# Normed rows moved to blocked tiles within SBUF, and transfers placed behind weight fetches, in a cross-attention and expert-FFN kernel

## The chip, the cores and the metric

One Trainium2 chip, one core. The metric is the device time of one execution in microseconds; the kernel before was timed in three runs. One profiled execution gives the page and the trace.

## What is computed

All in float32. Two steps, each added to x (8 batches of 1024 rows of 1024 numbers):

```python
def xattn(h, mem, mask):           # h = layernorm(x); mem: 8 x 64 x 1024
    scores = einsum('bsd,bmd->bsm', h, mem) / sqrt(D)
    attn = softmax(where(mask, scores, -1e30))
    return einsum('bsm,bmd->bsd', attn, mem)

def ffn(h, weight, lora_A, lora_B, router_w):   # h = layernorm(x)
    base = h @ weight.T                          # 1024 x 1024
    top2 = the two largest of softmax(h @ router_w.T), made to sum to 1   # 8 experts
    Ax = einsum('nd,erd->ner', h, lora_A)        # rank 16
    return base + einsum('ner,ne,eor->no', Ax, top2, lora_B) * 2

x = x + xattn(layernorm(x), ctx, mask)
x = x + ffn(layernorm(x), weight, lora_A, lora_B, router_w)
```

## The kernel before

The 8192 rows are 64 tiles of 128 rows. Two tiles make a pair, two pairs a quad. `first` does pairs 0 and 1 and prepares the weights; `quad(u)` is called for u = 2, 4, ... 30. Inside it, `u` and `v` are the pairs whose large product with the weights is made; `n`, `m` are the next two, whose attention, norm and turning are done meanwhile; `a`, `b` are the last two, to which the low-rank part is added before they are stored; `f`, `g` come after `n`, `m` and are loaded, turned and scored. `r` is a tile of a pair.

The large product is done with fewer block products, at two levels. A quad makes seven products, in the order 2, 5, 4, 1, 6, 7, 3 (`joint(i, u, ...)`), and each of them is seven parts of two matmuls 128x128 by 128x290 (four records in the profile, since each float32 matmul shows as two). The 34 columns beyond 256 carry a share of the low rank and the router. A part's result is read out of PSUM into T or xt by VectorE, or by ScalarE where `copy` says so (L906 to L946). `joint_sums` (L867) makes a product's operands on GpSimd (POOL); `t_add` (L835) adds T to xt there; `sums_1_2` (L711) makes the sums of a pair.

Three of the seven weight operands of a product are sums of weight blocks that lie in DRAM, in pieces of 290 KB. `fetch()` (L775) brings the next piece on SyncE's queue (SP) into one of four buffers (`q`), and `joint` calls it three times: after its second part, its fourth and its last. The order is fixed (L768), so that the fetches of product 5 bring two pieces of product 4 and one of product 1, those of product 4 two of product 1 and one of 6, those of product 6 two of product 7 and one of 3, and so on. The second part of a product needs its piece 4, the fourth part piece 2, the last part piece 3. In the trace the pieces are `q_w` and `q_t`, by the name of the weight block.

All DMAs are issued by SP, in the order of the program; the other engines follow the order of the program too (`manual_schedule`). What SP waits for holds up all behind it.

VectorE can transpose blocks of 32x32 alone. So rows that are to be turned must lie blocked: the tile's partitions 32q to 32q+31 hold column group q (256 columns) of the rows of all four row groups t. x is loaded a second time in this form (`xs`, `load_xs`, L115, four DMAs of 128 KB per tile) and turned by `att_turn_tile` (L444). The normed rows `h` (`f_rows`, L330, on ScalarE) are written to DRAM (`hd`, one DMA of 512 KB per tile) and read back blocked (`hs`, four DMAs of 128 KB per tile) by `norm_send` and `norm_fetch` (L589, L598), and `rt_turn_tile` (L619) turns them. `xs`, `h`, `hs` are tiles of one pool of four buffers of 4 KB per partition (`ring`, L66).

The attention memory of a batch serves four pairs. For every second quad, up to u = 22, a new one is read in blocked form (`load_ms`, L391, eight DMAs of 32 KB in runs of 128 bytes), turned and summed (`turn_mem`, L404) and centred (`centre_turned`, L412).

`turn_low_rank` (L695) turns the routed low-rank numbers of two pairs on TensorE: two transposes, a copy out of PSUM by ScalarE, two transposes, a copy; all four transposes write one bank. `lora_tile` (L952) adds them to xt by eight matmuls (`lo`) per pair. In a quad, SP and ScalarE are given:

- after product 2 and the attention of n and m: sums, squares and root of pair n (`f_sums`, `f_squares`, `f_std`), then `turn_low_rank`, then product 5 with `f_rows(n)` and its sending after the first part;
- `f_rows(m)`, the low rank of a and its stores, product 4, the low rank of b and its stores, load of f, product 1, load of g;
- product 6 with the turning of n, loads of `xs`, product 7 with the turning of m, loads of `xs`, product 3 with the turning of the xs of f; the xs of g are turned in product 2 of the next quad.

Of the kernel before, what the change touches and what calls it, by code (L numbers as in the profile page):

```python
# [17 lines left out]
P = 128  # L18
# [6 lines left out]
def kernel(  # L25
# [281 lines left out]
    def f_rows_steps(u: int):  # L307

        nm, std, of_f = fts.pop(u)
        rstd, nmr = of_f[:, 4], of_f[:, 5]  # L310

        def row(r: int):
            h = ring.tile([P, D], F32, tag="ring", name=f"h_{u}_{r}")
            hss.setdefault(u, []).append(h)
            nc.scalar.activation(
                halves(h), body(xts[u][r]), AF.Identity, bias=nmr[:, r, :], scale=rstd[:, r, :]
            )

        def one():
            nc.vector.reciprocal(rstd, std)  # L320
            tt(nmr, nm, rstd, ALU.mult)
            row(0)

        def two():
            row(1)
            norm_send(u)

        return one, two

    def f_rows(u: int, fetch: bool = True):  # L330
# [11 lines left out]
        norm_send(u, fetch)  # L342
# [48 lines left out]
    def load_ms(b: int):  # L391

        mt = memp.tile([P, KD, M], F32, tag="memT", name=f"memT_{b}_True", bufs=1)
        for q in range(4):
            for t in range(M // NB):
                nc.sync.dma_start(
                    out=mt[q * NB : (q + 1) * NB, :, t * NB : (t + 1) * NB],
                    in_=mem[b, t * NB : (t + 1) * NB, q * QD : (q + 1) * QD].rearrange(
                        "i (k c) -> i k c", c=NB
                    ),  # L400
                )
        mem_ts[b, True] = mt

    def turn_mem(b: int):  # L404

        mt = mem_ts[b, True]
        turn = mt.rearrange("p k (t i) -> p (k t) i", i=NB)
        nc.vector.transpose(turn, turn)
        mcs[b] = small.tile([P, M], F32, tag="of_k", name=f"of_k_{b}")
        nc.vector.tensor_reduce(mcs[b], mt.rearrange("p k m -> p m k"), AX.X, ALU.add)  # L410

    def centre_turned(b: int):  # L412

        of_k = mcs.pop(b)
        mt = mem_ts[b, True]
        means = bank_of(f"means_{b}")[:, :M]
        mm(means, ones, of_k, start=True, stop=True)
        tt(mt, mt, means.unsqueeze(1).to_broadcast([P, KD, M]), ALU.subtract)


    x_ts, scs, ps, pts, ros, hds, hss, rdens = {}, {}, {}, {}, {}, {}, {}, {}
# [167 lines left out]
    def norm_send(u: int, fetch: bool = True):  # L589

        hds[u] = dram.tile([2 * P, D], F32, tag="hd", name=f"hd_{u}")
        hs_in, hss[u] = hss[u], []
        for r in range(2):
            nc.sync.dma_start(out=hds[u][r * P : (r + 1) * P, :], in_=hs_in[r])
        if fetch:
            norm_fetch(u)

    def norm_fetch(u: int):  # L598
        for r in range(2):
            hs = ring.tile([P, 4, QD], F32, tag="ring", name=f"hs_{u}_{r}")  # L600
            load_blocked(hs, hds[u][r * P : (r + 1) * P, :])
            hss[u].append(hs)
# [277 lines left out]
    def joint(i: int, u: int, hooks, wide: int = HX, copy=None):  # L880
# [35 lines left out]
        def hook(step: int):  # L916
            for do in hooks.get(step, ()):
                do()
# [9 lines left out]
        fetch()  # L928
        read(v, 0, p4)
# [5 lines left out]
        fetch()  # L935
        read(u, 1, chain)
# [8 lines left out]
        fetch()  # L945
        tt(to(v), chain.unsqueeze(1).to_broadcast([P, 2, wide]), to(v), ALU.add)  # L946
# [29 lines left out]
    def first():  # L976
# [124 lines left out]
        load_xs(4)  # L1101
# [6 lines left out]
        f_rows(2)  # L1108
        low_rank_tile(1, 0)
# [6 lines left out]
        sum_3(1)  # L1116
        quarter_sums("t1", t1)
        load_ms(1)
# [20 lines left out]
        att_turn(4)  # L1139
# [4 lines left out]
        centre_turned(1)  # L1144
# [4 lines left out]
        end = joint_plain(2, 1, {0: lambda: product(1, 8)})  # L1149
# [6 lines left out]
        load_xs(5)  # L1156
# [3 lines left out]
        for _ in range(4):  # L1160
            fetch()
        x_stats(5)
# [12 lines left out]
    def quad(u: int):  # L1175
# [4 lines left out]
        far = f < NP  # L1180
        prev = u > 2
# [3 lines left out]
        next_mem = f + 2 < NP and (f + 2) % PPB == 0  # L1185
        vector, scalar = nc.vector.tensor_copy, nc.scalar.copy

        def nothing(*_):
            pass

        hooks = {}
        if more:
            att_sc([n, m])
            att_rstd(n)
            att_rstd(m)
            hooks[1] = [lambda: att_exp([n, m])]
        if far:
            load_xs(g) if not prev else nothing()
            if not prev:
                hooks[2] = [lambda: att_turn(f)]  # L1200
            hooks[3] = [lambda: att_turn_tile(g, 0)]
            hooks[5] = [lambda: att_turn_tile(g, 1)]
# [35 lines left out]
        if next_mem:  # L1238
            load_mask((f + 2) // PPB)
            load_ms((f + 2) // PPB)  # L1240
        if prev:
            turn_low_rank(a, b)

        hooks = {}
        if more:
            hooks[1] = [lambda: f_rows(n)]
        joint(5, u, hooks, wide, vector)
        if more:
# [3 lines left out]
            f_rows(m)  # L1252
# [3 lines left out]
        if prev:  # L1256
            for r in range(2):
                lora_tile(a, r)
                store(a, r)

# [3 lines left out]
        joint(4, u, {}, wide)  # L1264
        joint_sums(6, u)
        if prev:
            for r in range(2):
                lora_tile(b, r)
                store(b, r)
        if far:  # L1270
            load_xt(f)
# [3 lines left out]
        joint(1, u, {}, wide, scalar)  # L1275
# [4 lines left out]
        if far:  # L1280
            x_stats(f)
            load_xt(g)
        if not more:
            for r in range(2):
# [99 lines left out]
```

## Time and profile before

| what | value |
|---|---|
| median of three runs | 1369.92 us (1362.94 to 1375.46) |
| profiled execution, its own time | 1374.05 us |
| span in its trace | 1372.2 us |
| mean granted TensorE clock | 0.922 |
| TensorE matmuls busy | 84% of the span |
| VectorE, POOL, ScalarE busy | 57%, 56%, 41% |
| DMA traffic | 274.34 MB, 200 GB/s |

A row of the waits names the engine and line that waited, then what released it, the sum in us, how often and the longest. In the list of SP's queue SPq is SyncE issuing DMAs. `jc` and `j` are PSUM banks of the products, `lo` those of the low rank, `trw` that of the turned low rank, `L801` is the matmul of a block. The stretch from 645 to 728 us, one quad (u = 14) from the end of its readouts to the end of the next, is used throughout.

### The profile page before, as it was taken

Reading aid. Unit: us, or ns where it says so; the run is one execution under the profiler, and the core shown is the slowest. Engines: PE = TensorE matmul, PEld = TensorE weight load, DVE = VectorE, ACT = ScalarE, POOL = GpSimd, SP = SyncE. Lnnn points to the kernel's source line nnn. Section 1 sums busy time; section 2 is a strip of 40 time slices with the busy share of each in tenths; the row PEclk is TensorE's granted clock in tenths of the full one; section 3 lists DMA queues with packets and bytes.
Section 4 is the critical chain, followed back from the end, with each engine's and each line's share of the span. In section 5 each row is a group of like instructions: output and inputs, shape, how many; then the busy total and the mean of one; then the engine's idle time right before and its main releaser. Section 6 shows DMA issues by size and latency. Waiting matters only on the chain.

```text
span 1372.2 us, 16976 instructions
## 1 busy us (share of the span) xinstructions
PE 1151.1 (84%) x4968; PEld 791.7 (58%) x4968; DVE 787.5 (57%) x1829; ACT 555.9 (41%) x1116; POOL 761.7 (56%) x837
## 2 busy tenths in 40 slices
PE   8978788987888878888988888888888798878988
PEld 6444565655656646555665555656555565555766
DVE  6864456574664746647475464754647466363554
ACT  4663534434353253543345433354533445323110
POOL 0487364583644736556384554836448375463844
PEclk9998898998999999899899999989999899889999
DMA  9889483966839569394874839658395783827534
GB/s 221 212 257 277 151 245 113 306 157 196 254 105 305 143 188 274 107 310 124 262 220 151 270 99 309 180 174 273 108 299 148 223 263 107 269 70 240 143 118 127
DMA packets 218443, 274.34 MB, mean 200 GB/s; under 512 B 33392, under 2 KB 166512, under 8 KB 218352
## 3 DMA queue, kind: packets, MB, share of 16 engines
q1 hardware_dynamic: 218352, 273.26, 67.2%
q8 instruction: 41, 0.67, 0.2%
q14 instruction: 50, 0.41, 0.1%
HBM read 201.94 MB, written 71.25 MB: 199 GB/s over the span
## 4 chain that ended last, share of the span: by engine, by line
PE 46%; DMA 16%; DVE 11%; POOL 11%; ACT 9%; issue 3%; SPq 3%; DVEq 0%; ACTq 0%; POOLq 0%
PE j L801 20%; PE jc L801 18%; PE lo L791 7%; DMA q_w<-q_w 5%; DMA q_t<-q_t 5%; POOL xt L839 3%; ACT junk L296 3%; DVE xt L544 3%; DMA xt<-in_x_dram 2%; SPq L85 2%; DMA xs<-in_x_dram 2%; DVE xt L912 1%; DVE xs L448 1%; ACT junk L286 1%; POOL s L716 1%
## 5 line engine op out<-in xcount | busy, mean ns | idle before, releaser
L839 POOL TENSOR_TENSOR xt<-xt,T 128x580 f32<-128x580 f32 (+1 forms) x180 | 247.9, 1406 | 193.3 <-DVE T L912 193.3
L801 PE MATMUL jc<-q_t,s_j 128*128 128x290 f32 (+1 forms) x480 | 144.0, 423 | 60.6 <-DVE T L912 44.5
L912 DVE TENSOR_TENSOR T<-j,T 128x290 f32<-128x290 f32 (+1 forms) x180 | 76.0, 443 | 162.0 <-PE j L801 152.3
L801 PE MATMUL jc<-q_w,s_j 128*128 128x290 f32 (+1 forms) x360 | 115.4, 447 | 43.3 <-DMA q_w<-q_w 40.2
L801 PE MATMUL j<-w,s_j 128*128 128x290 f32 (+1 forms) x480 | 143.2, 422 | 8.2 <-DVE xt L912 6.5
L801 PEld LDWEIGHTS jc<-q_t,s_j 128*128 128x128 f32 x480 | 92.0, 197 | 98.1 <-DVE T L912 54.3
L875 POOL TENSOR_TENSOR s_j<-hA 128x256 f32<-128x256 f32 x30 | 22.2, 740 | 215.4 <-PE jc L801 215.4
L801 PEld LDWEIGHTS j<-w,s_j 128*128 128x128 f32 x480 | 95.9, 202 | 43.1 <-POOL s_j L876 10.4
L801 PEld LDWEIGHTS jc<-q_w,s_j 128*128 128x128 f32 x360 | 71.1, 205 | 73.6 <-issue 48.6
L801 PE MATMUL j<-t,s_j 128*128 128x290 f32 (+1 forms) x360 | 108.0, 424 | 0.0
L791 PE MATMUL lo<-lb_sb,axwt 128*128 128x512 f32 x240 | 107.8, 592 | 0.0
L510 ACT ACTIVATE s<-s,of_s 128x64 f32<-128x64 f32 x64 | 21.5, 337 | 200.5 <-DVE of_s L501 200.5
L912 DVE TENSOR_TENSOR xt<-j,xt 128x290 f32<-128x290 f32 (+1 forms) x180 | 78.1, 444 | 31.0 <-PE j L801 31.0
L339 ACT ACTIVATE h<-xt,of_f 128x1024 f32<-128x1024 f32 x60 | 71.2, 1234 | 55.2 <-DVE of_f L335 55.2
L910 ACT COPY T<-jc 128x290 f32<-128x290 f32 (+1 forms) x30 | 12.0, 400 | 199.2 <-PE jc L801 199.2
L544 DVE SCALAR_TENSOR_TENSOR xt<-ro,of_s,xt 128x512 f32<-128x512 f32 x128 | 86.2, 743 | 6.1 <-PE ro L538 5.9
L788 DVE TENSOR_TENSOR xt<-lo,xt 128x512 f32<-128x512 f32 x120 | 79.1, 685 | 12.4 <-PE lo L791 8.3
L286 ACT ACTIVATE junk<-xt 128x1024 uint8<-128x1024 f32 x60 | 63.4, 1057 | 54.9 <-DVE xt L544 54.0
L801 PEld LDWEIGHTS j<-t,s_j 128*128 128x128 f32 x360 | 71.5, 200 | 22.5 <-issue 1.8
L239 ACT ACTIVATE junk<-xt 128x1024 uint8<-128x1024 f32 x60 | 63.2, 1054 | 51.9 <-DMA xt<-in_x_dram 51.7
L703 PE MATMUL trw<-ident,axl 128*128 128x128 f32 x64 | 17.4, 363 | 75.0 <-ACT axwt L704 75.0
L538 PE MATMUL ro<-mem,s 64*128 64x512 f32 x256 | 72.0, 614 | 9.4 <-DVE xt L544 8.4
(209 smaller groups left out, 2418.3 us busy)
## 6 DMA issues: line engine op xcount, KB each, us to landing
q_t<-q_t SPq DMA_DIRECT2D x192, 290.0 KB, 4.3
q_w<-q_w SPq DMA_DIRECT2D x144, 290.0 KB, 4.4
xt<-in_x_dram SPq DMA_DIRECT2D x64, 512.0 KB, 6.8
out_dram<-xt SPq DMA_DIRECT2D x62, 512.0 KB, 5.3
xs<-in_x_dram SPq DMA_DIRECT2D x240, 128.0 KB, 4.0
hd<-h SPq DMA_DIRECT2D x60, 512.0 KB, 3.8
hs<-hd SPq DMA_DIRECT2D x240, 128.0 KB, 3.1
mem<-in_ctx_dram SPq DMA_DIRECT2D x16, 256.0 KB, 3.9
```

Of the source, the lines that this page charges most:

```text
L85: nc.sync.dma_start(out=dst[q * NB : (q + 1) * NB], in_=v[:, :, q * QD : (q + 1) * QD])
L239: nc.scalar.activation(nowhere, body(xts[u][r]), AF.Identity, accum_out=sm[:, r, :])
L286: nc.scalar.activation(nowhere, body(xts[u][r]), AF.Identity, accum_out=sm[:, r, :])
L296: nc.scalar.activation(nowhere, body(xts[u][r]), AF.Square, bias=nm[:, r, :], accum_out=ss[:, r, :])
L339: nc.scalar.activation(halves(h), body(xts[u][r]), AF.Identity, bias=nmr[:, r, :], scale=rstd[:, r, :])
L538: mm(ro, pts[u][rows, :], m[rows, ts(c, HB)], start=True, stop=True)
L544: nc.vector.scalar_tensor_tensor(xc, halves(ros.pop((u, c, r))), rdens[u][:, r : r + 1], xc, ALU.mult, ALU.add)
L788: tt(xc, halves(bank), xc, ALU.add)
L791: mm(bank, axwts[u][:, r, :], lb_sb[:, c0 : c0 + n], start=alone, stop=True, skip_group_check=True)
L801: mm(bank, a[:, k, :], w[:, k], start=(start and k == 0), stop=(k == n - 1), skip_group_check=True)
L839: nc.gpsimd.tensor_tensor(xc, xc, Ts[p][:, :, :wide], ALU.add)
L912: tt(t, bank, t, ALU.add)
```

## The change

- `norm_send` no longer goes through DRAM. A tile is moved from `h` to `hs` within SBUF by 16 DMAs of 32 KB, one for each row group t and column group q (32 partitions, a run of 1 KB in each). It is no longer part of `f_rows`; its place is given by hand.
- `joint` takes hooks "f1", "f2", "f3" behind its three fetches. Behind them now stand: the sending of n (product 5, f3) and of m (product 6, f1 and f2, a tile each); the stores of a (product 4) and b (product 1); the loads of xt (products 4, 1 and 6); the loads of xs (product 7 and, for the last tile, product 3); the load of a mask (product 2).
- `f_rows(n)` runs at hook 5 of product 5 instead of hook 1; `f_rows(m)` at hook 4 of product 4 instead of ahead of it.
- `turn_low_rank` runs after the first part of product 5 instead of ahead of it.
- The xs of f and the first tile of g are turned in product 3; only the second tile of g is turned in product 2.
- The memory is loaded with four DMAs in runs of 1 KB into a `ring` tile, turned in place in product 5 (hook 4), and centred into `memT` in product 4 (hook 3).
- In `first` the sending of pairs 2 and 3 and the loads of xs are reordered in the same manner.

The diff, cut to its core; the hooks of `quad` stand in the order of the products 2, 5, 4, 1, 6, 7, 3:

```diff
     def load_ms(b: int):
+        if b > 1:
+            t = ring.tile([P, D], F32, tag="ring", name=f"ms_{b}")
+        else:
+            t = x_tile(f"ms_{b}").rearrange("p j o -> p (j o)")
+        t = t[:, : M // NB * QD].rearrange("p (t c) -> p t c", c=QD)
+        load_blocked(t, mem[b])
+        mcs[b] = t.rearrange("p t (k i) -> p t k i", i=NB)
...
-    def norm_send(u: int, fetch: bool = True):
-        hds[u] = dram.tile([2 * P, D], F32, tag="hd", name=f"hd_{u}")
-        hs_in, hss[u] = hss[u], []
+    def norm_send_tile(u: int, r: int):
+        hs = ring.tile([P, 4, QD], F32, tag="ring", name=f"hs_{u}_{r}")
+        h = hss[u][r]
+        for t in range(4):
+            for q in range(4):
+                nc.sync.dma_start(
+                    out=hs[q * NB : (q + 1) * NB, t, :],
+                    in_=h[t * NB : (t + 1) * NB, q * QD : (q + 1) * QD],
+                )
+        hss[u][r] = hs
+
+    def norm_send(u: int):
         for r in range(2):
-            nc.sync.dma_start(out=hds[u][r * P : (r + 1) * P, :], in_=hs_in[r])
-        if fetch:
-            norm_fetch(u)
+            norm_send_tile(u, r)
...
         part(p4, d[:, HK:], q4, True)
         fetch()
+        hook("f1")
...
         part(chain, s2, q2, False)
         fetch()
+        hook("f2")
...
         part(chain, s3, q3, False)
         fetch()
+        hook("f3")
...
 def first():
         f_rows(2)
+        norm_send(2)
+        load_xs(4)
...
         att_scores([4], both)
-        load_xs(5)
+        norm_send(3)
         end = joint_plain(4, 1)
         end()
         store(1, 1)
         for _ in range(4):
             fetch()
+        load_xs(5)
...
 def quad(u):
-            hooks[3] = [lambda: att_turn_tile(g, 0)]
-            hooks[5] = [lambda: att_turn_tile(g, 1)]
+            do(hooks, 4, lambda: att_turn_tile(g, 1))
+        if next_mem:
+            do(hooks, "f1", lambda: load_mask((f + 2) // PPB))
...
+        hooks = {}
         if prev:
-            turn_low_rank(a, b)
-        hooks = {}
+            do(hooks, 0, lambda: turn_low_rank(a, b))
         if more:
-            hooks[1] = [lambda: f_rows(n)]
+            do(hooks, 5, lambda: f_rows(n))
+            do(hooks, "f3", lambda: norm_send(n))
+        if next_mem:
+            do(hooks, 4, lambda: turn_mem((f + 2) // PPB))
...
-            f_rows(m)
...
+        if prev:
+            do(hooks, "f1", lambda: store(a, 0))
+            do(hooks, "f2", lambda: store(a, 1))
+        if more:
+            do(hooks, 4, lambda: f_rows(m))
+        if next_mem:
+            do(hooks, 3, lambda: centre_turned((f + 2) // PPB))
+        if far:
+            do(hooks, "f3", lambda: load_xt(f, (0,)))
...
+        if far:
+            do(hooks, "f1", lambda: load_xt(f, (1,)))
+        if prev:
+            do(hooks, "f1", lambda: store(b, 0))
+            do(hooks, "f2", lambda: store(b, 1))
...
         if more:
-            hooks[1] = [lambda: rt_turn_tile(n, 0)]
-            hooks[4] = [lambda: rt_turn_tile(n, 1)]
+            do(hooks, 1, lambda: rt_turn_tile(n, 0))
+            do(hooks, 4, lambda: rt_turn_tile(n, 1))
+            do(hooks, "f1", lambda: norm_send_tile(m, 0))
+            do(hooks, "f2", lambda: norm_send_tile(m, 1))
+        if far:
+            do(hooks, "f2", lambda: load_xt(g, (0,)))
+            do(hooks, "f3", lambda: load_xt(g, (1,)))
...
+        if next_far:
+            do(hooks, "f1", lambda: load_xs(f + 2, (0,)))
+            do(hooks, "f2", lambda: load_xs(f + 2, (1,)))
+            do(hooks, "f3", lambda: load_xs(g + 2, (0,)))
...
-        if f + 2 < NP:
-            hooks[1] = [lambda: att_turn_tile(f + 2, 0)]
-            hooks[4] = [lambda: att_turn_tile(f + 2, 1)]
+        if next_far:
+            do(hooks, "f1", lambda: load_xs(g + 2, (1,)))
+            do(hooks, 1, lambda: att_turn_tile(f + 2, 0))
+            do(hooks, 3, lambda: att_turn_tile(f + 2, 1))
+            do(hooks, 5, lambda: att_turn_tile(g + 2, 0))
```

## The prediction

> **What bounds the kernel now.** The page comes first: the busy shares and the DMA rows.
>
> ```profile
> PE 1151.1 (84%) x4968; PEld 791.7 (58%) x4968; DVE 787.5 (57%) x1829; ACT 555.9 (41%) x1116; POOL 761.7 (56%) x837
> ...
> hd<-h SPq DMA_DIRECT2D x60, 512.0 KB, 3.8
> hs<-hd SPq DMA_DIRECT2D x240, 128.0 KB, 3.1
> ```
>
> TensorE is the bound, and what a change can win is its idle time. The list of waits says which waits come once in each quad:
>
> ```profile
> PE trw L703 <- ACT axwt L704: 75.0, 15, 5.7
> ...
> PE jc L801 <- DVE T L912: 44.5, 14, 3.2
> ...
> PE jc L801 <- DMA q_w<-q_w: 40.2, 15, 3.7
> ```
>
> Three waits, of 5.7, 3.1 and 2.4 us in a typical quad. The SyncE queue's own waits tell where the third comes from: SP stands still for ScalarE's rows and for the write to memory before it may read it back.
>
> ```profile
> SPq L594 <- ACT h L339: 199.5, 57, 19.3
> SPq L85 <- DMA hd<-h: 73.4, 31, 5.1
> ```
>
> The timeline of SP in the quad from 645 to 728 us shows it in place (start, length, issues):
>
> ```profile
> 640.73 3.65 SPq L396 DMA_DIRECT2D memT_True<-in_ctx_dram  x7
> 656.15 1.48 SPq L594 DMA_DIRECT2D hd<-h  x2
> 658.88 3.67 SPq L85 DMA_DIRECT2D hs<-hd  x8
> 662.65 0.85 SPq L778 DMA_DIRECT2D q_t<-q_t  x2
> 663.60 0.38 SPq L778 DMA_DIRECT2D q_w<-q_w  x1
> 665.56 1.45 SPq L594 DMA_DIRECT2D hd<-h  x2
> 669.62 3.64 SPq L85 DMA_DIRECT2D hs<-hd  x8
> 673.37 1.28 SPq L950 DMA_DIRECT2D out_dram<-xt  x2
> 674.73 2.25 SPq L778 DMA_DIRECT2D q_w<-q_w  x2
> ```
>
> The fetches of product 4 (674.73) could have gone from 666.5 on; they stand behind h, hd and hs, and product 1 waits 2.42 us for one at 680.35. Eight hs take 3.67 us: an issue every 0.47 us. This is the price on which all hangs.
>
> **The quad in numbers.** I count from 645.23, when the readouts end. In the timeline of PE product 5 ends at 16.0 us, product 1 at 40.8, product 7 at 58.2, product 3 at 65.3, the next readouts at 82.4. A part (four records, `L801 x4`) takes 0.98 us, the eight `lo` 3.43.
>
> **Part by part.**
>
> *Low rank inside product 5.* The second pair of `trw` waits for ScalarE's copy of the first (5.72 us), and ScalarE is busy with sums, squares and root of pair n until 651.08. That order stays, so the wait stays; only one part (0.98 us) moves into it. Taken: -1.0; bounds: 0 and -5.7.
>
> *One transposition of xs leaves product 2 for product 3.* VectorE there stands at 1.25 us and ends product 2 some 0.6 us behind PE (last add ends 720.03), with routing behind it. Taken -0.6, bounds 0 and -1.25. In product 3 it is covered by PE's new wait below; without that cover it costs up to 1.25.
>
> *Moves at nothing.* Stores, loads of xt and xs, and the mask keep their number; their places are in the walk. `f_rows` of n runs at hook 5 of product 5, and its rows (2.4 us on ScalarE) are done as the third fetch goes out. The memory: eight issues become four, at a place where SP then idles (644.4 to 656.2); its transposition and sum (0.70 + 1.06 us) go from product 6's end to product 5, where VectorE has gaps of 0.5 to 6 us. In its old place VectorE waited 3.05 us for POOL anyway, so it wins nothing. Without the gaps it costs 1.8 us in six quads.
>
> *The rows.* Per tile one hd and four hs issues become 16 issues of 32 KB: 64 in a quad for 20. Their step isn't in the trace. Above: the memory's 32 KB, 0.49 us with 256 runs in each; below: one issue alone takes 0.32, so 0.36 with its gap. From 256 runs to 128 the step falls only from 0.49 to 0.47, so I take 0.45 for 32 runs: 7.2 us for a tile. Their landing: 2.0 us, as memT's. Gone are SP's waits for hd, and 2 MB per quad of traffic; the DMA engines' room matters between 674 and 694 us only, where the DMA view shows up to 380 GB/s.
>
> One skill rule speaks against this. The memory's rows above are 32 KB too, and SP sends one each 0.49 us without waiting for the last. The Trainium skill (DMA: Bandwidth & Descriptors, section Bandwidth) tells to batch to 1 MiB and calls transfers under 64 KB descriptor-dominated, with 0.95 us at 64 KB, measured in loads from memory by another path. Taken as 16 times 0.95 us one after the other, an estimate from that page, a tile would cost 15.2 us and the sum below would rise by over 100 us. The overlap in the rows decides against it.
>
> *The walk* (us after the readouts; DMA landings are 2.8 after issue where the queue is short, as for the fetches at 711 to 719):
> - Product 5 ends at 15.0. SP issues its last fetch, then 32 pieces of n: 15.5 + 14.4 = 29.9. Only then come product 4's fetches. The first lands at 32.7; PE is there at 15.0 + 3.4 + 6.8 + 3.4 + 2.9 = 31.6. ScalarE is a little later still: its second row of m needs the buffer that n's last piece (31.4) frees, then 1.24 and a 0.40 copy: 33.1. Wait 1.5 us instead of 2.42, and no half clock (before: eight records in 3.7 us for 1.95). Product 1 ends at 37.0, 3.8 earlier.
> - Product 6: first fetch until 39.4, then 16 pieces of m. A DMA waits for the landing of the eighth before it (the issues use eight semaphores in turn). The stores, loads and fetches since 29.9 are 5.2 MB; at 380 GB/s the last lands at 44.6. So the eighth piece goes then, the 16th at 48.2, landed 50.2. POOL's chain (13.1 us from product 1's end to the released T, 685.8 to 698.9) ends at 50.1, so the wait of 3.1 us in product 7 stays about. VectorE: read 0.5, two transpositions 1.4, two reads 0.8; PE's last two parts 2.0: product 7 ends at 54.8.
> - The second tile of m takes the buffer that its first row gave up: it starts at 50.2, ends at 57.4. Then one xt (0.65), and at 58.1 product 6's third fetch, the piece w22 that product 3 needs in its second part. It lands behind the xt at 62.3. PE wants it at 55.8: a new wait of 6.5 us, and some 2.4 us of half clock after it (5.3 us at 0.5 after the wait of 5.72 cost 2.65).
> - Product 3 ends at 62.3 + 5.9 + 2.4 = 70.6, 5.3 later than before; the rest takes 17.1 - 0.6. Quad: 87.1 us for 82.4, +4.7.
>
> **Sum.** 13 quads x 4.7 = 61; the one without xt loads +2.5; six quads with a memory +1.5 each, since its tile holds one of four ring buffers until product 4 and the second tile of n waits for the first's landing: +9; in the first part 44 more issues (0 to +20, taken 6, as PE waited there for xs and for a fetch of 6.4 us already); last quad -1; the small waits for q_t (0.4 to 1.2 us in half of the quads) are in the new wait: -10. Together +67 on the profiled run's 1374 (span 1372.2, 2 around it; the median of the runs is 4 lower): about 1440.
>
> **Ends.** With 0.49 us and 300 GB/s the same walk gives 93.2 us a quad: +10.8, near 1540 with the first part's 20. With 0.36 us, product 1 doesn't wait, the second tile ends at 52.4, product 3's piece lands at 57.3 and the quad takes 81.4: -1.0; without the wait for the buffer 76.8: -5.6.
>
> **Rivals.**
> 1. *Faster: cheap issues.* At 0.36 us the two old waits shrink more than the new one costs. It decides below 0.38 us (between 81.4 and 87.1). For it: the first of a series takes 0.32. Against it: every second one takes 0.43 and a gap of 0.05, whatever its runs. Between -1.0 and -5.6 for 14 quads: 1360 to 1296, in the middle 1328. Chance 0.14.
> 2. *Nothing to tell:* about 0.38 us, or the second tile of m not held by its buffer: gains of 4.4 us before product 6 pay for the wait in product 3. 1374, within 1360 to 1384. Chance 0.10.
> 3. *Much slower:* the full burst at 300 GB/s and 0.49 us: the new wait nears 10 us in each quad and clock halves with it. 1500 to 1540. Chance 0.10.
> 4. *My forecast*, pieces of 0.42 to 0.47: 1384 to 1500, middle 1440. Chance 0.66. The low rank not doing what it is placed for is inside it: a wait of over 4 us on L703 stays.
>
> The range leaves out about one in ten on each side: 1352 to 1500; the likeliest's own is 1384 to 1500. Under 1% (13.7 us) a measurement of this kernel can't tell from none. Faster 0.14, same 0.10, slower 0.76.
>
> **What would show it.** In the new SP timeline: 32 issues in a row after product 5, 0.45 us apart (right) or under 0.38 (wrong); a fetch of q_w at the end of product 6 some 20 us after its start. In the waits: `PE jc L801 <- DMA q_w` at product 3 of 5 us and more; L703 still at 4 to 5; the wait in product 1 below 2; `SPq L594` and `hd` gone. What would make it wrong: a step below 0.38, a second buffer at hand, or pieces that overtake the large transfers.

## The result, and the profile after

| | before | after |
|---|---|---|
| median on the same chip (four runs each) | 1366.43 us | 1745.03 us (1742.3 to 1750.31) |
| ratio, with its 95% interval | | 1.2765 (1.2685 to 1.2846) |
| profiled execution, its own time | 1374.05 us | 1750.31 us |
| span of its trace | 1372.2 us | 1748.3 us |
| mean granted TensorE clock | 0.922 | 0.840 |

The change makes the kernel slower by 28%. The forecast of 1440 us had the sign right and the size wrong: its range ended at 1500. Some executions of one and the same kernel take a per cent or two longer than the rest, and ratios here compare the others alone, so a ratio need not be that of the two medians.

The page of the kernel after: busy shares, the chain by engine and by line, and the issues of the rows.

```profile
PE 1251.3 (72%) x4968; PEld 841.8 (48%) x4968; DVE 781.5 (45%) x1829; ACT 554.2 (32%) x1116; POOL 761.5 (44%) x837
...
SPq 33%; PE 23%; DMA 19%; DVE 10%; ACT 7%; issue 6%; POOL 3%; DVEq 0%; ACTq 0%; POOLq 0%
SPq L573 28%; PE j L780 11%; DMA xs<-in_x_dram 9%; PE jc L780 8%; DMA q_t<-q_t 3%; DMA q_w<-q_w 2%; DVE xt L522 2%; ACT junk L296 2%; SPq L757 2%; SPq L85 1%; DMA w<-in_w_t_dram 1%; PE lo L770 1%; SPq L125 1%; DVE xt L928 1%; ACT L304 1%
...
hs<-h SPq DMA_DIRECT2D x960, 32.0 KB, 1.8
```

The chain by engine of the kernel before:

```profile
PE 46%; DMA 16%; DVE 11%; POOL 11%; ACT 9%; issue 3%; SPq 3%; DVEq 0%; ACTq 0%; POOLq 0%
```

VectorE, ScalarE and POOL do the same work as before, in us. What has changed is who sets the end: a third of the chain is SyncE issuing DMAs, 28% of the span on L573 alone, the line that sends the normed rows. The traffic fell from 274.34 to 242.97 MB, as the change intends, and the rate from 200 to 139 GB/s: over the span, bytes are not what is short.

The list of waits of the kernel after shows TensorE's waits that belong to a quad, and ahead of them those of VectorE and ScalarE for the pieces (`hs<-h`) and for xs:

```profile
DVE hA L91 <- DMA hs<-h: 174.6, 30, 10.3
ACT h L316 <- DMA hs<-h: 168.2, 22, 9.7
...
DVE xs L426 <- DMA xs<-in_x_dram: 163.6, 40, 9.6
...
PE j L780 <- DMA q_w<-q_w: 116.4, 14, 10.2
...
PE jc L780 <- DMA q_w<-q_w: 75.3, 17, 15.3
...
PE trw L682 <- ACT axwt L683: 59.7, 15, 4.7
```

Here L780 is the matmul of a block (L801 before) and L682 the turning of the low rank (L703 before). The 116.4 us, 14 times, are product 3's wait for w22, which the kernel before did not have. The 4.7 of `trw` is what the forecast said would stay of 5.7.

A quad now takes 108 to 111 us, where it took 82 to 87. The same quad as in the prediction, u = 14, lies from 722.7 to 830.9 us after. In the view by windows, the columns are the busy times of PE, PEld, DVE, ACT and POOL, the clock, the DMA share and GB/s; first the kernel before, then the kernel after.

```profile
645.30:727.70 82.40, 70.02 (x304) 48.57 (x304) 49.87 (x114) 34.64 (x71) 47.19 (x52) 0.92 0.67 204
```

```profile
722.70:830.90 108.20, 77.64 (x301) 52.34 (x301) 47.42 (x114) 35.57 (x72) 47.09 (x52) 0.84 0.54 143
```

The quad is 25.8 us longer: 7.6 of it is TensorE busier with the same matmuls, at a lower clock, and 18.2 is TensorE idle (30.6 us instead of 12.4). The timeline of SP shows why, with start, length and number of issues:

```profile
736.84 20.43 SPq L573 DMA_DIRECT2D hs<-h  x32
757.37 0.53 SPq L757 DMA_DIRECT2D q_w<-q_w  x1
...
770.07 11.37 SPq L573 DMA_DIRECT2D hs<-h  x16
781.53 0.53 SPq L757 DMA_DIRECT2D q_t<-q_t  x1
782.16 10.00 SPq L573 DMA_DIRECT2D hs<-h  x16
792.21 0.64 SPq L125 DMA_DIRECT2D xt<-in_x_dram  x1
792.95 0.56 SPq L757 DMA_DIRECT2D q_w<-q_w  x1
...
803.18 0.34 SPq L757 DMA_DIRECT2D q_w<-q_w  x1
```

The 32 pieces of n take 20.43 us, which is 0.63 us a piece, where I had taken 0.45. The fetch that product 1 wants leaves only at 757.37. The pieces of m hold the queue from 770 to 792, and w22 leaves at 792.95. The timeline of PE has the waits that follow, in brackets:

```profile
728.79 0.69 PE L682 MATMUL trw<-ident,axl 128*128 128x128 f32 x2 [4.69 <-ACT axwt L683]
760.50 2.27 PE L780 MATMUL jc<-q_w,s_j 128*128 128x290 f32 x4 [7.42 <-ACT T L889]
780.19 1.25 PE L780 MATMUL jc<-q_t,s_j 128*128 128x290 f32 x4 [2.73 <-DVE T L891]
785.26 1.39 PE L780 MATMUL j<-t,s_j 128*128 128x290 f32 x4 [2.85 <-DVE T L891]
797.40 2.27 PE L780 MATMUL j<-q_w,s 128*128 128x290 f32 x4 [7.28 <-DMA q_w<-q_w]
806.80 1.22 PE L780 MATMUL j<-w,s_j 128*128 128x290 f32 x4 [2.07 <-DVE xt L891]
810.95 2.27 PE L780 MATMUL jc<-q_w,s_j 128*128 128x290 f32 x4 [2.93 <-issue]
```

The second wait is put down to a copy of ScalarE, because the copy came last: ScalarE stood 8.90 us in `h` (L316) for the ring buffer that n's last piece gave up, and its copies of T stand behind that row. The fetch issued at 757.37 comes at about the same time, so the burst causes this wait twice. In the fourth, VectorE's queue stood 2.97 us for m's pieces (until 783.10) with two additions to T behind it. In the sixth it stood 7.90 us for xs, whose loads left behind w22. The last one is put down to "issue", but it is VectorE's as well: its addition of the bank that TensorE wants stood behind the turning of the second tile of xs, and TensorE starts 0.10 us after it has ended, as in all 14 waits of that row (33.6 us).

```profile
809.26 1.25 DVE L426 STREAM_TRANSPOSE xs<-xs 128x1024 f32<-128x1024 f32 x1 [2.60 <-DMA xs<-in_x_dram]
810.43 0.42 DVE L891 TENSOR_TENSOR xt<-jc,xt 128x290 f32<-128x290 f32 x1
```

Four records take up to 2.27 us after a long wait, at a granted clock of 0.50 (797.4 to 803.0), and 1.14 otherwise; this is what half clock means here.

The burst of pieces also leaves the DMA engines idle and fills them afterwards. While n's pieces go out (736 to 754 us) the engines are busy for 23% of the time, at 63 GB/s. From 797.4 to 803.0, when the loads that stood behind m's pieces are under way, the same view shows them full (a share of 1.06), and xs lands 7 to 9 us after its issue; in the same quad before it took 3 to 5.

### The profile page after: what moved, and what is told of

The parts are those of the page before. It is cut to its first block, busy times and chain, and to the rows that moved or that the text cites. A ratio compares the mean times of both kernels' runs of the same rounds, so it can differ in the third digit from the quotient of the medians.

```text
span 1748.3 us, 17766 instructions
## 1 busy us (share of the span) xinstructions
PE 1251.3 (72%) x4968; PEld 841.8 (48%) x4968; DVE 781.5 (45%) x1829; ACT 554.2 (32%) x1116; POOL 761.5 (44%) x837
## 2 busy tenths in 40 slices
DMA packets 208337, 242.97 MB, mean 139 GB/s; under 512 B 29168, under 2 KB 164080, under 8 KB 208240
## 4 chain that ended last, share of the span: by engine, by line
SPq 33%; PE 23%; DMA 19%; DVE 10%; ACT 7%; issue 6%; POOL 3%; DVEq 0%; ACTq 0%; POOLq 0%
SPq L573 28%; PE j L780 11%; DMA xs<-in_x_dram 9%; PE jc L780 8%; DMA q_t<-q_t 3%; DMA q_w<-q_w 2%; DVE xt L522 2%; ACT junk L296 2%; SPq L757 2%; SPq L85 1%; DMA w<-in_w_t_dram 1%; PE lo L770 1%; SPq L125 1%; DVE xt L928 1%; ACT L304 1%
## 5 line engine op out<-in xcount | busy, mean ns | idle before, releaser
L780 PE MATMUL jc<-q_w,s_j 128*128 128x290 f32 (+1 forms) x360 | 138.2, 518 | 153.4 <-DMA q_w<-q_w 75.3
L780 PE MATMUL j<-w,s_j 128*128 128x290 f32 (+1 forms) x480 | 169.1, 483 | 36.7 <-DVE xt L891 31.2
L780 PE MATMUL jc<-q_t,s_j 128*128 128x290 f32 (+1 forms) x480 | 155.0, 449 | 48.3 <-DVE T L891 41.6
L239 ACT ACTIVATE junk<-xt 128x1024 uint8<-128x1024 f32 x60 | 63.4, 1057 | 393.7 <-DMA xt<-in_x_dram 393.6
L780 PEld LDWEIGHTS jc<-q_w,s_j 128*128 128x128 f32 x360 | 82.1, 240 | 196.2 <-ACT T L889 120.8
L316 ACT ACTIVATE h<-xt,of_f 128x1024 f32<-128x1024 f32 x60 | 72.7, 1237 | 303.8 <-DMA hs<-h 168.2
L780 PEld LDWEIGHTS j<-w,s_j 128*128 128x128 f32 x480 | 109.4, 232 | 83.7 <-POOL s_j L854 16.3
L426 DVE STREAM_TRANSPOSE xs<-xs 128x1024 f32<-128x1024 f32 x60 | 74.0, 1239 | 163.6 <-DMA xs<-in_x_dram 163.6
L780 PEld LDWEIGHTS jc<-q_t,s_j 128*128 128x128 f32 x480 | 99.0, 212 | 87.4 <-DVE T L891 47.4
L694 POOL TENSOR_TENSOR s<-hA,hB 128x512 f32<-128x512 f32 x31 | 40.6, 1308 | 211.5 <-DVE hB L91 211.5
L780 PE MATMUL j<-t,s_j 128*128 128x290 f32 (+1 forms) x360 | 110.2, 431 | 18.5 <-DVE T L891 18.4
L91 DVE STREAM_TRANSPOSE hA<-hs 128x512 f32<-128x512 f32 x60 | 42.6, 709 | 175.1 <-DMA hs<-h 174.6
L780 PE MATMUL j<-q_w,s 128*128 128x290 f32 (+1 forms) x60 | 32.8, 700 | 116.4 <-DMA q_w<-q_w 116.4
L780 PEld LDWEIGHTS j<-t,s_j 128*128 128x128 f32 x360 | 70.9, 200 | 46.1 <-issue 26.9
L447 PE MATMUL sct<-xs,memT_True 128*64 128x128 f32 x960 | 59.2, 281 | 29.3 <-DVE xs L426 29.3
```

Source lines behind the costliest of these rows:

```text
L91: nc.vector.transpose(dst.rearrange("p k (t i) -> p t k i", i=NB), src.rearrange("p t (k i) -> p t k i", i=NB),)
L239: nc.scalar.activation(nowhere, body(xts[u][r]), AF.Identity, accum_out=sm[:, r, :])
L316: nc.scalar.activation(halves(h), body(xts[u][r]), AF.Identity, bias=nmr[:, r, :], scale=rstd[:, r, :])
L426: nc.vector.transpose(v, v)
L447: mm(sct[r * M : (r + 1) * M, j, :].rearrange("m (t i) -> m t i", i=NB), mt[:, k, :], x_ts[u][r][:, k], start=(k == 0), stop=(k == KD - 1),)
L780: mm(bank, a[:, k, :], w[:, k], start=(start and k == 0), stop=(k == n - 1), skip_group_check=True)
```

## The experiments

Theory A: SyncE's queue is bound by the number of its issues, and the fetches come late because they stand behind the pieces. Rival B: the new places of the other work are the fault, whatever carries the rows. Rival C: the bytes moved within SBUF get in the way of the engines. All ratios are against runs of the kernel before on the same chip.

**The same places, through DRAM.**

```diff
+        hd = dram.tile([P, D], F32, tag="hd", name=f"hd_{u}_{r}")
+        nc.sync.dma_start(out=hd, in_=hss[u][r])
...
-                nc.sync.dma_start(
-                    out=hs[q * NB : (q + 1) * NB, t, :],
-                    in_=h[t * NB : (t + 1) * NB, q * QD : (q + 1) * QD],
-                )
+        load_blocked(hs, hd)
```

> The changed kernel with all its places kept; only a tile's way differs: it goes through DRAM again (one write of 512 KB, four blocked reads of 128 KB), so five issues stand where 16 stood, and the queue waits once for the write to land. Theory A (SyncE's queue: 64 issues x 0.633 us = 40.5 us per quad hold the fetches back): a tile holds the queue some 4.9 us (0.35 issue, 2.7 landing, 4 x 0.47) instead of 10.1; the wait in product 1 and the one in product 3 (7.3 us each) go nearly to 0, and the time falls to 1290 to 1350 us. Theory B (the places are wrong, rows are sent too late): it stays above 1600. Theory C (moves within SBUF slow the other transfers): it falls as under A, so this run doesn't tell A from C.

Measured: 1485.68 us, ratio 1.0757 (1.0723 to 1.0790). Quads took 90 to 95 us. The places alone explain at most these 7.6%, so B is refuted as the main cause; A's number was missed as well. SP's own waits say by what:

```profile
SPq L85 <- DMA hd<-h: 236.1, 60, 6.3
```

In a queue in program order, the wait for a landing is paid by all that stands behind: 236 us in 60 waits, 3.9 each, where the kernel before had 73.4. So this is not the change with the issues taken out: it has a cost of its own.

**Four DMAs per tile within SBUF.** The same bytes from SBUF to SBUF in 4 DMAs. Each row stays in its partition, so this kernel leaves out the blocked order; the work on the engines is the same.

```diff
-        h = hss[u][r]
-        for t in range(4):
-            for q in range(4):
...
+        h = hss[u][r].rearrange("p (t c) -> p t c", c=QD)
+        for q in range(4):
+            nc.sync.dma_start(
+                out=hs[q * NB : (q + 1) * NB], in_=h[q * NB : (q + 1) * NB]
+            )
```

> The changed kernel, but a tile is copied within SBUF by four DMAs (32 partitions, four runs of 1 KB in each) that keep every row in its partition. The same bytes, places and waits with a quarter of the issues. Left out: the rows aren't brought into blocked order, so the product is made of rows in a wrong order. Theory A: a tile holds the queue some 2 us; the waits of 7 us go, 1280 to 1340 us. Theory C (bytes moved within SBUF are what hurts): above 1600. Theory B: above 1600.

Measured: 1344.83 us, ratio 0.975 (0.9703 to 0.9798). That is 5 us above A's range. Both 7 us waits are gone, and quads take 80 to 83 us. The bytes, the engines and the places are those of the kernel after, so B and C fall and the number of issues is left; an issue of this form is no cheaper (a step of 0.636 us here and 0.633 in the kernel after). In the list of TensorE's waits `trw` is first again:

```profile
PE trw L680 <- ACT axwt L681: 59.7, 15, 4.7
PE jc L778 <- DVE T L889: 43.8, 14, 3.2
```

**Eight per tile**, as above but in halves: is the price linear in the number?

```diff
+        for t in (slice(0, 2), slice(2, 4)):
             for q in range(4):
...
+                    out=hs[q * NB : (q + 1) * NB, t], in_=h[q * NB : (q + 1) * NB, t]
```

> As the run with four DMAs per tile, but with eight (32 partitions, two runs of 1 KB in each). Left out, as there: the rows aren't brought into blocked order. Theory A, every issue counts (queue time on the chain): four gave 0.975 of the kernel before and 16 gave 1.277, 0.025 per issue and tile; eight give about 1.075, 1470 to 1500 us. Rival D, a threshold (a tile's issues cost nothing as long as they fit between two fetches; 8 x 0.63 = 5.1 us do, in a product of 6.9): 0.96 to 1.0, at most 1380 us.

Measured: 1441.86 us, ratio 1.0438 (1.0365 to 1.0512), between the two cases. From four to eight issues a tile the ratio rises by 0.017 for each, from 8 to 16 by 0.029. So it is neither linear nor a step. For 60 tiles one issue more is 60 times 0.633 = 38 us of queue time, and 0.017 and 0.029 of before are some 24 and 40 us: the first issues are partly hidden, the last are paid about in full. Half clock comes along: TensorE's busy time is 1155.5 us with four, 1182.8 with eight and 1251.3 with sixteen.

**What sets the step.** Series of 16 issues one behind the other, with nothing else in the program, each of another form. The first and the third:

```python
for t in range(4):
    for q in range(4):
        dma(out=a[rows(q), t, :], in_=flat[rows(t), q * QD : (q + 1) * QD])   # flat: SBUF
...
        dma(out=c[rows(q), t, :], in_=hd[rows(t), q * QD : (q + 1) * QD])     # hd: DRAM
```

> The disputed price by itself: two rounds of ten series of 16 DMAs, all other work left out, so that the outputs are not computed. To read: the time from issue to issue in each series. If one run per partition makes an issue dear: series 1, 2, 3, 4, 8 at 0.6 us and 5, 6 at 0.47. If it is dear because both ends lie in SBUF: 1, 2, 6, 7, 8 at 0.6 and 3, 4, 5, 9 at 0.47. If few partitions make it dear: 7 and 9 (128 partitions) below 0.5 and 1 to 6 and 8 at 0.6. If it was only company on the chip (other transfers in flight): 1 at 0.47 or less.

The timeline of SP in this kernel. In order: 32 runs of 1 KB within SBUF to other partitions, the same to the same partitions, from DRAM, to DRAM, then 32 x 4 x 256 bytes, 128 x 256 bytes and 32 x 4 KB within SBUF, and 128 x 256 bytes from DRAM.

```profile
88.32 10.01 SPq L61 DMA_DIRECT2D a<-src  x16
98.38 10.97 SPq L65 DMA_DIRECT2D b<-src  x16
109.39 7.92 SPq L69 DMA_DIRECT2D c<-hd  x16
117.35 7.58 SPq L73 DMA_DIRECT2D out_dram<-src  x16
...
135.78 10.31 SPq L81 DMA_DIRECT2D e<-src  x16
146.14 10.25 SPq L85 DMA_DIRECT2D f<-src  x16
156.44 10.12 SPq L89 DMA_DIRECT2D g<-src  x16
166.60 7.71 SPq L93 DMA_DIRECT2D f<-hd  x16
```

Sixteen issues take 10.0 to 11.0 us when both ends lie in SBUF, and 7.6 to 7.9 when one end is in DRAM. The median step is 0.633 to 0.653 us for the first kind and 0.463 to 0.474 for the second; 32 or 128 partitions, runs of 256 bytes to 4 KB and the bytes make no difference of note. That ScalarE's queue issued the first form every 0.669 us is not its own price: it wrote the tile that SyncE's second series had just written, and each of its issues started within 0.1 us after the landing there. The run with the pieces of m on ScalarE's queue, below, has 0.641. The one left out, 32 x 4 x 1 KB from DRAM, had issues of 0.31 us but a step of 0.603: each writes over what the fourth before it wrote, and from the fifth on they waited for those landings (127.80, next issue 127.82).

**The same 16 issues, read from DRAM.** Each tile is written to DRAM right after its rows are made; the 16 pieces stand where they stand in the kernel after.

```diff
+    def norm_write(u: int):
...
+        for r in range(2):
+            hd = dram.tile([P, D], F32, tag=f"hd{r}", name=f"hd_{u}_{r}")
+            nc.sync.dma_start(out=hd, in_=hss[u][r])
+            hss[u][r] = hd
...
     def norm_send(u: int):
+        norm_write(u)
...
+            do(hooks, "f3", lambda: norm_write(m))
```

> The changed kernel with the same number of issues in the same places, 16 of 32 KB per tile, but read from DRAM, into which each tile is written before by one issue (n behind product 5, m behind product 4). In the series by themselves a step took 0.633 us with both ends in SBUF and 0.464 with one in DRAM. If the step is what my sum had too small: a tile holds the queue 7.4 us instead of 10.1, n waits some 3 us more for its write; the time falls to 1.10 to 1.20 of before, about where the forecast's walk had put it with 0.45 to 0.47 (1.05) and what came on top. If the number of issues sets the time whatever the step: it stays at 1.25 or more.

Measured: 1669.77 us, ratio 1.2088 (1.2017 to 1.2159), just above the first case. The 32 pieces of n take 14.7 us instead of 20.4, and the waits of products 1 and 3 shrink:

```profile
704.00 14.73 SPq L579 DMA_DIRECT2D hs<-hd  x32
731.96 11.75 SPq L579 DMA_DIRECT2D hs<-hd  x16
744.22 7.57 SPq L579 DMA_DIRECT2D hs<-hd  x16
```

```profile
721.74 2.27 PE L787 MATMUL jc<-q_w,s_j 128*128 128x290 f32 x4 [5.33 <-DMA q_w<-q_w]
757.05 2.27 PE L787 MATMUL j<-q_w,s 128*128 128x290 f32 x4 [4.84 <-DMA q_w<-q_w]
```

The pieces have the step that I forecast with (0.46), and quads take 102 to 106 us, not 87. But it isn't the kernel of the forecast, since the writes cost too: from 700.16 to 704.00 the queue issues those of n and waits for one to land, and those of m take 1.84 us in product 4. So the longer step explains at least some 0.07 (1.2765 less 1.2088) of the 0.277 that the change costs, a quarter. In us a quad that is 4.8 (109.0 less 104.2 on average); with the 5.7 us of queue time that the writes take, if all of it reaches TensorE, it would be some 10, an estimate from these rows. The rest is in the quad's other terms, below.

**The pieces of m on ScalarE's queue.**

```diff
-    def norm_send_tile(u: int, r: int):
+    def norm_send_tile(u: int, r: int, by=nc.sync):
...
-                nc.sync.dma_start(
+                by.dma_start(
...
-            do(hooks, "f1", lambda: norm_send_tile(m, 0))
-            do(hooks, "f2", lambda: norm_send_tile(m, 1))
+            do(hooks, "f1", lambda: norm_send_tile(m, 0, nc.scalar))
+            do(hooks, "f2", lambda: norm_send_tile(m, 1, nc.scalar))
```

> The changed kernel, but the 32 pieces of pair m (in product 6) are issued by ScalarE; those of n stay with SyncE. Theory A: SyncE's fetches in product 6 go out in time, the wait of 7.3 us in product 3 and those of 2 to 3 us after it go, the wait in product 1 (7.4) stays: about 11 us less in 14 quads, 1570 to 1620 us, unless ScalarE's 32 x 0.6 = 19 us make its own work (36 us per quad) late. Theory C: the bytes are the same, it stays within 3% of 1745.

Measured: 1655.94 us, ratio 1.2001 (1.1965 to 1.2037): between the two, 36 us above A's range. Product 3's wait for w22 is gone, which shows that it came from SP's queue. But the rows of m come no earlier by the other queue. The 32 issues stand in ScalarE's order of work and hold it for 22 us, which the expectation had named as its exception, and the next in line takes over:

```profile
732.32 21.98 ACTq L573 DMA_DIRECT2D hs<-h  x32
```

```profile
PE j L780 <- DVE T L891: 69.0, 13, 7.9
PE jc L780 <- POOL s L694: 68.2, 14, 5.8
PE jc L780 <- ACT T L889: 61.3, 8, 8.0
```

VectorE waits for the pieces, POOL for VectorE, and TensorE for both. Behind the late fetch stand late rows.

**The low rank alone.** The kernel before, with `turn_low_rank` at hook 0 of product 5, as in the change.

```diff
+        hooks = {}
         if prev:
-            turn_low_rank(a, b)
...
+            hooks[0] = [lambda: turn_low_rank(a, b)]
```

> The kernel before with one edit: the low rank is turned after the first part of product 5 instead of ahead of it. If ScalarE's sums, squares and root of pair n set the end of the wait, as in the changed kernel (4.7 us left of 5.7), it wins one part, 1.0 us in 14 quads: 0.985 to 0.995 of before. If the place inside the product hides the turning: the wait and its half clock go, 5 to 8 us a quad, 0.92 to 0.95.

Measured: 1353.88 us, ratio 0.9712 (0.9640 to 0.9785), below the 0.985 to 0.995 expected for this case. The wait is the 4.7 us of the forecast:

```profile
PE trw L703 <- ACT axwt L704: 59.7, 15, 4.7
```

75.0 us have become 59.7, 1.0 for each of 15, and the span is 13.2 us shorter (1359.0). The measured 2.9% is more than the traces explain. This profiled execution (1360.79 us) is the slowest of its six, which go down to 1336.07 and of which the ratio takes the three fastest, and the runs of the kernel before on that chip lie between 1370.89 and 1395.46; the rest of the difference stays open.

**The same turning at hook 6**, with the rows of n behind it: ahead of the product's last part, where ScalarE's sums of n are done.

```diff
+        hooks = {6: []}
         if prev:
-            turn_low_rank(a, b)
...
+            hooks[6].append(lambda: turn_low_rank(a, b))
         if more:
-            hooks[1] = [lambda: f_rows(n)]
+            hooks[6].append(lambda: f_rows(n))
```

> The kernel before with one edit: the low rank is turned at hook 6 of product 5, with f_rows of n behind it. Against hook 0 (0.971 of before) the wait for ScalarE (4.7 us) and the half clock after it (2.6) go, but the rows of n are not there much earlier, and the fetches for product 1 stand behind the sending of m as before, so that its wait grows by 1 to 2 us: 0.91 to 0.95 of before. If the fetches take all of it back: 0.96 or more.

Measured: 1334.62 us, ratio 0.9648 (0.9593 to 0.9703). The wait of `trw` falls to 6.9 us in the whole run (0.5 each), but part of it comes back: the rows of n leave later, and TensorE meets waits of 2.9 us in product 4 for VectorE's additions (`PE j L801 <- DVE xt L788`, 38.0 us, 13 times) and of up to 2.5 for `q_t`. By its number that is the second case of the expectation, but not by its reason: against hook 0 TensorE's waits for fetches fell, from 44.7 to 30.8 us in all, and it is VectorE that takes part of the gain back.

**Through DRAM, written early, read a product later** (e7 in the expectations below). From the first experiment: `norm_write(n)` behind product 5's third fetch, its read behind product 4's first two; m written in product 4, read in product 1; the loads moved to make room.

```diff
-            do(hooks, "f3", lambda: norm_send(n))
+            do(hooks, "f3", lambda: norm_write(n))
...
+            do(hooks, "f1", lambda: norm_read(n, 0))
+            do(hooks, "f2", lambda: norm_read(n, 1))
+            do(hooks, 4, lambda: f_rows(m))
+            do(hooks, "f3", lambda: norm_write(m))
...
+            do(hooks, "f1", lambda: norm_read(m, 0))
+            do(hooks, "f2", lambda: norm_read(m, 1))
```

> The changed kernel with the rows through DRAM, written (one issue a tile) as soon as they are there and read (four issues a tile) a product later, so that the queue never waits for a landing: n written behind product 5, read in product 4; m written behind product 4, read in product 1; stores of b, loads of xt and xs a step earlier or later to fit. Theory A: the waits in product 1 and product 3 both go, the 2 to 3 us for xs in products 3 and 2 too; left are 4.7 us for the low rank and 3 for T: about 77 to 79 us a quad, 0.93 to 0.96 of before. Rival: with the rows' 4 MB per quad back on the DMA engines the fetches land late after product 4, and it is no better than 0.98.

Measured: 1392.59 us, ratio 1.0071 (1.0034 to 1.0109); A is missed, and the number is the rival's. 7.6% are back to 0.7%, but SP's waits hold a new one, for VectorE:

```profile
SPq L85 <- DVE T L892: 51.4, 14, 5.0
...
SPq L85 <- DMA hd<-h: 33.8, 17, 2.7
```

In one quad the queue stands still from 691.18. The write of m's first tile lands at 693.29, and the read still goes out only at 697.38, as VectorE ends the turning of n's first tile (697.36): the read needs n's ring buffer. A fetch stands behind, and product 6 waits 3.8 us for it. So the order of the queue is to blame for most of the wait, not full DMA engines as the rival has it; the last run below carries the same bytes without it.

**Both: early write, and the low rank at hook 6** (e8).

```diff
-            do(hooks, 0, lambda: turn_low_rank(a, b))
+            do(hooks, 6, lambda: turn_low_rank(a, b))
...
-            do(hooks, 5, lambda: f_rows(n))
+            do(hooks, 6, lambda: f_rows(n))
```

> As e7, and the low rank is turned at hook 6 of product 5, after six of its seven parts, with f_rows of n behind it. ScalarE is through with the sums by then: the wait of 4.7 us and the half clock after it (2.6) fall to one copy, 0.5 us: 6 to 7 us a quad below e7, 0.85 to 0.89 of before. If instead POOL's chain or VectorE's reading of product 5 ends last in that stretch, less than 3 us a quad come: above 0.91.

Measured: 1316.95 us, ratio 0.9515 (0.9445 to 0.9586). The ratio is in the second case, because the run before it (e7) had come out above its own expectation; the gain, 5.4 us a quad (75.6 in 14), lies between the two cases. Against the run before it the low rank brings 5.4%, more than the wait itself (59.7 us become 6.9, 3.8% of 1392.59); TensorE's busy time falls as well, from 1159.1 to 1129.6 us with the same matmuls, while the mean granted clock rises from 0.926 to 0.954. The wait for `q_t` in product 6 stays at 61.4 us in all.

**And the queue spread.** The expectation puts the queue's wait in product 1 down to the landing of m's write; by the row above that explains its first 2 us and n's ring buffer the other 4. m is read in product 6, when n's buffers are free; the loads of xt and xs and one store are spread over products 1, 6, 7 and 3, and xs is turned later. The hooks of product 6:

```diff
-            do(hooks, "f1", lambda: load_xt(g, (0,)))
-            do(hooks, "f2", lambda: load_xt(g, (1,)))
-        if next_far:
-            do(hooks, "f3", lambda: load_xs(f + 2, (0,)))
+            do(hooks, "f1", lambda: norm_read(m, 0))
+            do(hooks, "f2", lambda: norm_read(m, 1))
+        if prev:
+            do(hooks, "f1", lambda: store(b, 1))
+        if far:
+            do(hooks, "f3", lambda: load_xt(g, (0,)))
         joint(6, u, hooks, wide)
```

> As e8, with the transfers spread: m is read a product later (behind product 6's fetches, when its write has long landed), loads of xt and xs and a store of b each one to three fetches later, the xs of g turned in product 2 as in the kernel before. In e7 and e8 the queue waited some 7 us in product 1 for m's write to land, and product 6 4 to 6 us for a fetch. If that wait was the queue's: it goes, some 4 us less in 14 quads than e8, 0.89 to 0.92 of before. If the DMA engines are full in products 4 to 6 whatever the order: another fetch comes late instead, 0.94 or more.

Measured: 1256.31 us, ratio 0.9089 (0.9033 to 0.9144): as expected, and faster than both kernels. Quads take 73 to 78 us. The first places in TensorE's waits:

```profile
PE jc L781 <- DVE T L892: 43.8, 14, 3.5
PE jc L781 <- issue: 25.2, 31, 3.7
PE j L781 <- DVE xt L892: 17.7, 14, 2.7
```

No fetch is among them; the waits put down to "issue" start again 0.10 us after a read by VectorE in each of the 31 cases. What stays is product 7's wait for POOL's chain, which all kernels here have.

Not tried: the kernel before with the 16 pieces alone, at its own places. m's rows and n's blocked tiles then hold all four ring buffers at once, and none is left for m's blocked tiles.

## Why the prediction was wrong, step by step

**The step that failed** is "so I take 0.45 for 32 runs". It measured 0.633, beyond both of its bounds (0.36 and 0.49). I had read the price of an issue as one of its runs, since the rows of before differed in runs (256 and 128, 0.49 and 0.47). The rows shared what counts: one end in DRAM. The trace of before held not one transfer from SBUF to SBUF, so the nearest row was no bound. Rival 1, cheap issues, fell with it. A second step failed beside it: the walk ends at w22 and puts what stands behind it at nothing.

The rule that I weighed and set aside, the Trainium skill (DMA: Bandwidth & Descriptors, section Bandwidth), gave by an estimate 15.2 us a tile and over 100 us more; measured were 10.1 us a tile, between the two. "Over 100" was short of its own working: 8.0 us more a tile are 448 us in 4 tiles and 14 quads. Its sum came nearer than mine, though not by its reckoning of one transfer after the other: pieces landing after 1.84 us left every 0.63.

Put into the old walk, 0.633 adds 32 times 0.183 = 5.9 us for n, which makes product 1's wait 1.5 + 5.9 = 7.4 (measured 7.42), and as much for m: 87.1 + 11.7 = 98.8 us a quad for 108.2 measured. So by the walk the mis-sized step is 11.7 of the 21.1 us that the quad was missed by. The trace agrees as to the place: w22's part starts 74.7 us after the readouts (797.40 less 722.70) where the walk had 62.3, so 12.4 us are lost by then and 8.7 behind it. The run with the step of 0.46 bounds it more loosely, between 4.8 and some 10 us a quad:

| TensorE in the quad, us | before | forecast | after |
|---|---|---|---|
| wait in `trw` | 5.72 | 4.7 | 4.69 |
| product 1's wait | 2.42 | 1.5 | 7.42 |
| product 7's wait for T | 3.1 | 3.1 | 2.73 |
| product 7, VectorE held by m's pieces | 0 | 0 | 2.85 |
| product 3, w22 | 0 | 6.5 | 7.28 |
| product 3, two tiles of xs late | 0 | 0 | 2.07 + 2.93 |
| busy | 70.02 | 70.7 | 77.64 |

The forecast's busy time is before's plus the 2.4 of half clock that it gave product 3, less the 1.75 that it took away in product 1.

- *Low rank, -1.0 a quad, the wait stays:* right, 75.0 to 59.7 us, in the change and by itself.
- *One transposition leaves product 2, -0.6:* about right. From product 3's end to the end of the readouts it was 17.1 us and is 17.9 (813.0 to 830.9), of which some 1.9 are half clock.
- *Moves at nothing:* wrong for xs. Their loads stood in the queue behind w22, landed 7 to 9 us after their issue, and cost 5.0 us in this quad. The walk ended at w22 and did not ask what stood behind it.
- *The walk:* its places were right (a burst after product 5, w22 behind both tiles of m, a new wait in product 3). Product 1's wait was to shrink and tripled. The pieces of m were followed only up to w22, not to VectorE's queue, where additions stand behind the turning: 2.85 us.
- *Half clock:* 2.4 us in one place were forecast; +7.6 us of busy time came, since five waits, of 2.85 to 7.42 us, brought slow matmuls after them (four records in up to 2.27 us); the sixth, of 2.73, did not. It doesn't go with the longer step alone: with issues of 0.46 us from DRAM the quad from 685 to 789 us has TensorE busy for 79.67 us.
- *First part, +6 (0 to +20):* +64 us up to the first low-rank transposes of u = 4 (224.8 to 288.5 us). The 32 pieces of pair 3 (126.29 to 146.58) stand ahead of the loads of xs that the scores need: that wait grew from 2.04 to 28.35 us. This is the worst-sized term outside the quads.
- *Gone are the waits for `hd` and 2 MB of traffic a quad:* right, and worth little: with both gone and four issues a tile the ratio is 0.975, and the low rank alone had 0.971.

Sum of the traces: +63.7 us to the third turning of the low rank, 11 full quads of +25.5 (83.6 to 109.0 on average, from turning to turning) = +280, and +32 in the rest: +376, the difference of the spans. The rival "much slower", 1500 to 1540, came nearest to what happened, halved clock and all, and stopped short with 0.49 us as its worst step. The range ended where that rival began.

The experiments leave the cause settled in kind: the number of issues (four a tile: 0.975; sixteen: 1.277, the same bytes and places), their price with both ends in SBUF (at least a quarter of the loss), and late pieces and late xs on the engines' own queues. How the rest divides between the step, what stood behind w22 and half clock was not measured by itself.

## What to carry to other kernels

Count the issues on each queue in the stretch that matters, times the step of that very kind of transfer, and if no row of the trace has both of its ends in the same kind of memory, measure a short series first: a bound from a row that differs in another respect is none. In a queue in program order, follow a burst past the first victim, to every load, fetch and engine queue behind it, and add the half clock that each new wait leaves behind it. Fewer bytes brought nothing here, where the DMA engines had room over the span (a share of 0.67 in the quad before, 0.54 after); few issues, no waits for landings in the queue, and a turning put where its engine is free brought 9%.

## What the runs showed of the hardware

- Issues on SyncE's queue went out every 0.63 to 0.65 us with both ends in SBUF, for 256 bytes to 4 KB a run and for 32 or 128 partitions, and every 0.46 to 0.47 with one end in DRAM, for runs of 256 bytes and 1 KB; on ScalarE's queue every 0.64 with both ends in SBUF.
- A piece of 32 KB within SBUF landed 1.84 us after its issue in the median, so three or so were under way at a time: the series was bound by the issuing, not by the transfers.
- After five waits of 2.85 to 7.42 us in a quad, four matmul records took 2.14 to 2.27 us for 1.14, at a granted clock of 0.5, and the quad's mean clock fell from 0.92 to 0.84. In the kernel before a wait of 2.42 us was enough (four records in 2.00 and 2.09 us). The best kernel, at 0.95 in its quad, gained by the clock as well as by the waits.
